# A two-layer graph attention kernel: reordering the first part and where Wr1 and the first residual products live

## The chip, the cores and the metric

The kernel runs on one core of one Trainium2 chip. Its time is the device time of one launch in microseconds (us), and the time of a kernel is the median over its runs. TensorE (PE) multiplies matrices; VectorE (DVE), ScalarE (ACT) and GpSimd (POOL) compute elementwise; SyncE (SP) only issues transfers. All have instruction queues of their own, which run in order.

## The reference

A graph has N = 3125 nodes with 768 features and E = 53125 edges, sorted by destination, with a self loop at every node.

```
h  = relu(layernorm(x))
# layer 1: 4 heads of 256
xl = h @ W1                                        # N x 1024
e  = leaky_relu((xl.a_src1)[src] + (xl.a_dst1)[dst], 0.2)   # per head
al = softmax of e over the edges that share a dst
g1 = segment_sum(xl[src] * al, dst) + b1
h1 = relu(layernorm(g1) * gamma1 + beta1) + (h @ Wr1 + br1)
# layer 2: the same with one head of 768 and W2, Wr2
out = x + layernorm(gat(h1)) * gamma2 + beta2 + (h1 @ Wr2 + br2)
```

## The kernel before, in words

Nodes are cut into 25 tiles of P = 125. Since the edges are sorted, the edges of a tile are a contiguous piece of the list; each tile gets S = 2304 slots, 18 chunks of 128, from its start in the list. `in_order` does the work in stages; `any_order` behind it is a fallback that runs only for a list that is not sorted. The Tile framework decides the order of instructions on each engine by priorities and inserts the waits; a buffer that is used again makes its new user wait for the old one.

1. `edge_list` (L188). The list `d_i` is loaded as 125 x 425. For each of 25 tiles DVE compares (L206) and ACT sums (L207), so that `cnt` holds how many edges lie below the tile; one product (L214) adds over partitions and gives `starts` (L219). The same function makes 16-bit copies of the list in HBM (`dst16_d`, and `slo16_d` for the source node modulo 125).
2. `fold` (L289). The attention vectors are folded into W1: POOL multiplies a 128-row chunk of W1 by a vector (L294), ACT sums over each head (L298) into `wa1`, so that h @ wa1 gives the node's attention terms.
3. `windows` (L236). For each tile SP reads its start and issues three transfers: destinations and sources as 32-bit numbers (`wd`, `ws`, L248 and L250) and 16-bit destinations (`k16`, L252). Seven tiles at a time are cast (L255) and transposed on PE (L257) into slot layout (L258). Then come gather indices, `hi_s` (source divided by 125) and `keep`.
4. Node tiles. Statistics (L313, L315, the square root on ACT L318, L321), normalisation, six transposes on PE (L570), ReLU into `h0` (L572), the next rows fetched, six products with `wa1` (L577, "alphas"), copied to `asad1` (L579).
5. `softmax` (L327) works in slot layout. Per tile it makes one-hot matrices on DVE from broadcast lists `bd` and `bs` (L359, L362, L365, L367), picks terms with PE (L377, L385), and then does segment maxima and sums by scans over rows. Meanwhile PE multiplies h0 by W1 (L588), ACT copies to `row` (L590), and SP stores `table1` and `h0T_d` (the transposed h0, by groups of four tiles).
6. Layer 1, in the pools "w2", "g1" and "e1". SP loads Wr1 (`wr1`, L601), the bias as two parts (`parts_of`, L149: load `v`, DVE splits off `lo`, SP stores it into row 1 of `b_r`, L164; four steps for 1024 columns), W2, and `h0k` (L614) from `h0T_d`. `residual(0)` (L624) computes the first group's residual h @ Wr1 and stores it to `r1T_d`. Then `sums` (L460) gathers one row of `table1` per slot (L477), weights it on ACT and DVE (L495, L496), adds by one-hot products on PE (L500, L512) over the bias product (L472), and ends each tile with `z` (L523). The fold of W2 (L294, L300) and `residual(1)` to `residual(6)` are handed to it as `later()`, a step per chunk.
7. Softmax and sums of layer 2 in the same manner; neither is touched except that both layers share the functions.

## Time and profile before

| what | value |
|---|---|
| runs | 2603.16, 2606.36, 2614.51 us; median 2606.36 |
| profiled execution | 2586.37 us, span 2584.5 us |
| mean granted PE clock of it | 0.936 |
| busy: PE, DVE, POOL, ACT | 2271.2, 1887.8, 1313.7, 1311.2 us |
| moved by DMA | 638.09 MB, mean 247 GB/s |
| first transpose of a node tile | 65.06 us |
| last copy of alphas | 144.22 us |
| first softmax product | 174.52 us |
| `residual(0)` on PE | 555.19 to 597.9 us |
| `z` of the first tile of layer 1 | 631.1 us |

How to read it: each engine's busy time is the sum of its instructions; PE's weight loads (PEld) run beside its products. In a line of the timeline the first two numbers are the start and the length in us, then come engine, line and operation, what is written from what, the size, how many (x), and in brackets how long the engine stood idle before it and which event ended that. A line of windows gives, for a stretch, its length and the busy time of PE, PEld, DVE, ACT and POOL with the number of instructions, then the granted clock of PE, the DMA share and GB/s.

### The profile page before, as it was taken

The numbers are of one execution on the slowest core, as the hardware profiler recorded it, in microseconds if no ns is written. First come the engines' busy times: TensorE is split into PE (matmuls) and PEld (weight loads), VectorE is DVE, ScalarE is ACT, GpSimd is POOL, SyncE is SP. The second block draws the span as 40 slices with busy tenths as digits, with TensorE's granted clock in tenths as the row PEclk, the third lists the DMA queues.
The fourth block names the chain that finished last, engine by engine and source line by source line (L and its number), as shares of the span: only waits on it lengthen the run. The fifth ranks groups of instructions, "written<-read, shape, count | busy, mean of one in ns | idle before, by whom it ended". The sixth has DMA issues, their size and how long they took to land. (4 is left out here: it accounts for less than half of the span.)

```text
span 2584.5 us, 35850 instructions
## 1 busy us (share of the span) xinstructions
PE 2271.2 (88%) x11226; PEld 1494.1 (58%) x11226; DVE 1887.8 (73%) x4289; ACT 1311.2 (51%) x2834; POOL 1313.7 (51%) x1007
## 2 busy tenths in 40 slices
PE   0969999949999999999999997768998889899786
PEld 0846654415666666666666675554575666566554
DVE  3559996027888988888888897785167768777776
ACT  5313321116788878888788894001044444444443
POOL 5100000047667667666676771002067778777875
PEclk9989999969999999999999998768999999999888
DMA  4228721177888888888888896773178988888886
GB/s 153 85 91 296 253 87 58 52 253 244 282 288 314 302 309 309 285 317 298 314 305 282 317 339 233 272 262 129 52 239 298 311 300 294 285 286 279 295 281 225
DMA packets 185428, 638.09 MB, mean 247 GB/s; under 512 B 31215, under 2 KB 50036, under 8 KB 184334
## 3 DMA queue, kind: packets, MB, share of 16 engines
q0 software_dynamic: 104032, 420.88, 47.7%
q1 hardware_dynamic: 76484, 202.08, 22.5%
q10 hardware_dynamic: 4714, 12.75, 1.4%
q8 instruction: 92, 1.51, 0.2%
q14 instruction: 106, 0.87, 0.1%
HBM read 566.11 MB, written 69.49 MB: 246 GB/s over the span
## 5 line engine op out<-in xcount | busy, mean ns | idle before, releaser
L477 POOL DMA_INDIRECT g<-table,idx_s x900 | 1196.8, 1330 | 1130.9 <-DVE oh L488 415.4
L495 ACT ACTIVATE hi<-g,al 128x256 fp32r<-128x256 f32 (+1 forms) x1925 | 970.9, 576 | 598.0 <-PE pa L500 275.0
L496 DVE SCALAR_TENSOR_TENSOR g<-g,al,hi 128x256 fp32r<-128x256 f32 (+1 forms) x1925 | 987.4, 564 | 126.8 <-ACT hi L495 124.4
L500 PE MATMUL pa<-hi,oh 128*125 128x512 f32 (+1 forms) x1450 | 581.0, 482 | 17.8 <-ACT hi L495 9.7
L500 PE MATMUL pa<-g,oh 128*125 128x512 f32 (+1 forms) x1450 | 459.4, 394 | 48.9 <-DVE g L496 48.4
L500 PEld LDWEIGHTS pa<-hi,oh 128*125 128x125 f32 x1450 | 270.5, 194 | 192.6 <-ACT hi L495 76.2
L500 PEld LDWEIGHTS pa<-g,oh 128*125 128x125 f32 x1450 | 269.7, 193 | 125.6 <-DVE g L496 86.2
L624 PE MATMUL pr<-h0k,wr 128*128 128x500 f32 (+1 forms) x672 | 300.7, 545 | 1.0 <-DMA h0k<-h0T_d 1.0
L717 PE MATMUL pr<-wr,h 128*125 128x384 f32 x800 | 299.3, 513 | 0.0
L677 PE MATMUL p<-w,h1T 128*125 128x384 f32 (+1 forms) x800 | 295.7, 489 | 1.8 <-DVE h1T L668 1.8
L512 PE MATMUL pa<-g,w 128*125 128x384 f32 (+1 forms) x900 | 291.8, 456 | 3.8 <-ACT w L510 3.0
L588 PE MATMUL pm<-w,h 128*125 128x512 f32 x600 | 274.7, 605 | 0.0
L512 PEld LDWEIGHTS pa<-g,w 128*125 128x125 f32 x900 | 171.7, 194 | 85.1 <-issue 27.8
L488 DVE TENSOR_SCALAR oh<-iota_f,rel_s 128x128 fp32r<-128x128 f32 x775 | 199.0, 286 | 20.1 <-PE pa L500 18.9
L717 PEld LDWEIGHTS pr<-wr,h 128*125 128x125 f32 x800 | 153.8, 197 | 92.1 <-issue 16.0
L677 PEld LDWEIGHTS p<-w,h1T 128*125 128x125 f32 x800 | 150.0, 188 | 72.8 <-DVE h1T L668 2.2
L588 PEld LDWEIGHTS pm<-w,h 128*125 128x125 f32 x600 | 110.0, 191 | 118.8 <-issue 118.8
L624 PEld LDWEIGHTS pr<-h0k,wr 128*128 128x128 f32 x672 | 124.9, 192 | 66.6 <-issue 22.8
L377 PE MATMUL pq<-tabs,ohs 125*128 125x100 bf16 (+1 forms) x2700 | 110.6, 198 | 43.4 <-DVE ohs L365 41.8
L377 PEld LDWEIGHTS <-ohs 125*128 125x128 bf16 x2700 | 105.5, 102 | 61.1 <-DVE ohs L365 54.3
L518 DVE TENSOR_TENSOR iso<-ao,node_f 125x1 f32<-125x1 f32 x50 | 7.8, 156 | 160.1 <-DMA ao<-alo_d,at_last 160.1
L590 ACT ACTIVATE row<-pm 125x512 f32<-125x512 f32 x50 | 29.8, 597 | 169.7 <-PE pm L588 159.2
(173 smaller groups left out, 1710.8 us busy)
## 6 DMA issues: line engine op xcount, KB each, us to landing
bd<-dst_d SPq DMA_DIRECT2D x50, 576.0 KB
bs<-slo_d SPq DMA_DIRECT2D x50, 576.0 KB
g<-table,idx_s POOLq DMA_INDIRECT x900, 5.9
r1T_d<-rt SPq DMA_DIRECT2D x100, 125.0 KB
r1t<-r1T_d SPq DMA_DIRECT2D x25, 500.0 KB
h1T_d<-h1T SPq DMA_DIRECT2D x25, 500.0 KB
h<-h1T_d SPq DMA_DIRECT2D x25, 500.0 KB
own<-table SPq DMA_DIRECT2D x24, 512.0 KB
```

The lines of the kernel that those rows point to most:

```text
L377: nc.tensor.matmul(q[:, j], ohs[:P, (j0 + j) * 128:(j0 + j + 1) * 128], tabs[:, i], start=(i == 0), stop=(i == 2))
L477: nc.gpsimd.indirect_dma_start(out=gf, out_offset=None, in_=table[:, :], in_offset=bass.IndirectOffsetOnAxis(ap=idx_s[:, c:c + 1], axis=0))
L488: nc.vector.tensor_scalar(oh, iota_f, rel_s[:, c:c + 1], None, op0=OP.is_equal)
L495: nc.scalar.activation(hi[:, cs], gf[:, cs], AF.Copy, scale=a)
L496: nc.vector.scalar_tensor_tensor(g[:, cs], gf[:, cs], a, hi[:, cs].bitcast(F32), op0=OP.mult, op1=OP.subtract)
L500: nc.tensor.matmul(pa[:, i, :f], oh[:, :P], t[:, i * f:(i + 1) * f], start=False, stop=(j == J - 1 and t is g))
L512: nc.tensor.matmul(pa[:, o // f, o % f:o % f + n], w[:, o // cols, :], gf[:, o:o + n], start=False, stop=(j == J - 1 and (o + n) % f == 0))
L588: nc.tensor.matmul(pm, h0[gi][:, k, o:o + P], w1[:, k, i * 512:(i + 1) * 512], start=(k == 0), stop=(k == NK1 - 1))
L590: nc.scalar.activation(row[:, i * 512:(i + 1) * 512], pm, AF.Copy)
L624: nc.tensor.matmul(pm[:, :nb * P], wr1[:, k, m * 128:(m + 1) * 128], loaded[gi, k][:, :nb * P], start=(k == 0), stop=(k == NK1 - 1))
L677: nc.tensor.matmul(pm[:, :n], hT[:, k, :], w2[:, k, o:o + n], start=(k == 0), stop=(k == NK2 - 1))
L717: nc.tensor.matmul(pm[:, :384], h1[:, k, :], wr2[:, k, i * 384:(i + 1) * 384], start=False, stop=(k == NK2 - 1))
```

## The change

- The counts: one DVE instruction with a running sum (`accum_out`) per tile instead of a comparison on DVE and a sum on ACT.
- Four node tiles (`EARLY = 4`) are written ahead of the rest of the list work: their rows x0 and x1 are fetched ahead of the list, W1 is loaded half by ACT's and half by POOL's queue, eight row buffers instead of twelve. `transposed` and `alphas` are separate functions; alphas lag four tiles behind.
- `windows` stands ahead of `fold` in the program, takes sources from a 16-bit copy `src16_d`, and transposes 25 x 128 pieces, 18 per list, with two transfers per tile.
- `folded` gives the two vectors and one or two product buffers in one tile. For layer 1 that tile is in the room "wr1" of pool m1; the softmax's scratch (`scr`) and then Wr1 itself take the same room. Inside the softmax `pick`, `ohh`, `le`, `xs` and `fw` are views of the scratch, and `alo` is a view of `own`.
- `residual(0)` is replaced by products straight from `h0[0]` behind the table's products, with `copy_residual` for its ACT pass and stores; group 0 is neither stored to `h0T_d` nor read back.
- The pools w2, g1 and e1 are opened with `reuse_waits="tile"`.

```
@@ edge_list
+        s16 = ep.tile([P, F], I16, name="s16")
+        nc.vector.tensor_copy(s16, s_i)
+        nc.sync.dma_start(src16_d.rearrange("(p f) -> p f", f=F), s16)
...
-            nc.vector.tensor_scalar(less, d16, float(b * P), None, op0=OP.is_lt)
-            nc.scalar.activation(less, less, AF.Copy, accum_out=cnt[:, b:b + 1])
+            nc.vector.tensor_scalar(less, d16, float(b * P), 0.0, op0=OP.is_lt, op1=OP.add,
+                                    accum_out=cnt[:, b:b + 1])
@@ windows
-                for k in range(n):
-                    st = start_of(b0 + k)
-                    nc.sync.dma_start(wd[k * J:(k + 1) * J, :],
-                                      dst[ds(st, S)].rearrange("(j p) -> j p", p=128))
-                    nc.sync.dma_start(ws[k * J:(k + 1) * J, :],
-                                      src[ds(st, S)].rearrange("(j p) -> j p", p=128))
-                    nc.sync.dma_start(k16[b0 + k:b0 + k + 1, :], dst16_d[ds(st, S)][None, :])
...
+            for b in range(NB):
+                st = start_of(b)
+                nc.sync.dma_start(k16[b:b + 1, :], dst16_d[ds(st, S)][None, :])
+                nc.sync.dma_start(s16[b:b + 1, :], src16_d[ds(st, S)][None, :])
+            for t, to in ((k16, dst_s), (s16, src_s)):
+                tf = ep.tile([NB, S], F32, name="tf")
+                nc.vector.tensor_copy(tf, t)
+                pt = pe.tile([128, 512], F32, name="pe")
+                for j in range(J):
+                    nc.tensor.transpose(pt[:, j * NB:(j + 1) * NB], tf[:, j * 128:(j + 1) * 128], ident[:NB, :NB])
...
@@ folded, fold
+        t = tmp.tile([128, 2 + room, heads * cols], F32, tag=tag, name="ab")
...
-                t = tmp.tile([128, heads, cols], F32, name="at", bufs=1 + act)
+                t = abs_[2 + m % (len(abs_) - 2)]
@@ softmax
+                first = scr()
...
-                xs = sr.tile([R, S], F32, name="xs")
-                fw = sr.tile([R, S], F32, name="fw")
+                rows = scr() if scr else sr.tile([128, 2 * S], F32, name="rows")
+                xs, fw = rows[:R, :S], rows[:R, S:2 * S]
@@ layer 1, before the table
-            for k in range(NK1):
-                nc.scalar.dma_start(w1[:, k, :], W1[k * 128:(k + 1) * 128, :])
...
+                    for b in range(2):
+                        fetch(b)
+                    listed = edge_list(ep, pp)
+                    next(listed)
+                    for k in range(NK1):
+                        (nc.scalar, nc.gpsimd)[k % 2].dma_start(w1[:, k, :], W1[k * 128:(k + 1) * 128, :])
+                    for b in range(2, AHEAD):
+                        fetch(b)
+                    abs1 = folded(mp, H, C1, a_src1, a_dst1, "wr1", 2)
+                    for b in range(EARLY):
+                        transposed(b)
+                    for _ in listed:
+                        pass
+                windows(pp)
+                for _ in fold(abs1, w1, NK1, H, C1, wa1, True):
+                    pass
+                for b in range(EARLY, NB):
+                    transposed(b)
+                    alphas(b - EARLY)
+                for b in range(NB - EARLY, NB):
+                    alphas(b)
@@ the table and behind it
+                wr1 = mp.tile([128, NK1, HC], F32, tag="wr1", name="wr1")
+                for k in range(NK1):
+                    nc.sync.dma_start(wr1[:, k, :], Wr1[k * 128:(k + 1) * 128, :])
...
-                    if b % GB == GB - 1 or b == NB - 1:
+                    if gi and (b % GB == GB - 1 or b == NB - 1):
                         nc.sync.dma_start(h0T_d[gi][:, :, :o + P], h0[gi])
+                for m in range(NK2):
...
+                        nc.tensor.matmul(pm[:, :GB * P], wr1[:, k, m * 128:(m + 1) * 128], h0[0][:, k, :],
+                                         start=(k == 0), stop=(k == NK1 - 1))
+                    copy_residual(0, rt, pm, m, GB)
...
-            for k in range(NK1):
-                load(0, k)
-            abs2 = folded(wp, 1, C2, a_src2, a_dst2)
-            for _ in residual(0):
-                pass
+            for k in range(NK1):
+                load(1, k)
+            abs2 = folded(wp, 1, C2, a_src2, a_dst2, "ab", 1)
```

## Prediction

> **What bounds the kernel now.** I read the page first, then busy time by stage (windows), then the list of waits and the timeline at each place where TensorE stands still. L-numbers are those of the kernel before.
>
> ```profile
> PE 2271.2 (88%) x11226; PEld 1494.1 (58%) x11226; DVE 1887.8 (73%) x4289; ACT 1311.2 (51%) x2834; POOL 1313.7 (51%) x1007
> PE   0969999949999999999999997768998889899786
> PEclk9989999969999999999999998768999999999888
> ```
>
> PE is busy 88% of the span. A digit stands for 64.6 us. The low ones ahead of layer 1 are the first (0 to 65 us), the third (129 to 194) and the ninth (517 to 582). So the kernel is PE-bound with holes, and a change of the first part can shorten holes. The stages in numbers (columns: stretch, sum of its length, busy PE, PEld, DVE, ACT, POOL, granted clock, DMA share, GB/s):
>
> ```profile
> 0.00:25.00 25.00, 0.00 (x0) 0.00 (x0) 13.73 (x36) 4.49 (x12) 10.13 (x17) 1.00 0.89 299
> 25.00:65.00 40.00, 0.25 (x2) 0.09 (x2) 9.21 (x37) 32.83 (x139) 23.17 (x10) 1.00 0.17 60
> 145.00:175.00 30.00, 15.79 (x57) 7.09 (x55) 12.58 (x33) 0.00 (x0) 0.00 (x0) 0.81 0.17 57
> 500.00:525.00 25.00, 14.59 (x35) 6.04 (x33) 2.53 (x11) 3.06 (x7) 4.81 (x4) 0.88 0.35 121
> 525.00:550.00 25.00, 1.18 (x2) 0.49 (x2) 8.55 (x25) 6.60 (x16) 10.61 (x11) 0.50 1.02 353
> 700.00:1400.00 700.00, 700.00 (x2527) 456.79 (x2526) 593.38 (x1656) 575.52 (x1465) 472.61 (x329) 1.00 0.87 303
> ```
>
> Three holes: 65 us at the start, about 14 us before 175, about 40 us after 515. From 700 to 1400 PE is full, so a us taken out ahead of that comes off the end. What ends each hole (timeline):
>
> ```profile
> 37.55 23.17 POOL L294 TENSOR_TENSOR at<-w,ab 128x1024 f32<-128x1024 f32 x10 [13.01 <-issue]
> 64.08 0.16 DVE L321 RECIPROCAL bn_rs<-bn_sd 125x1 f32<-125x1 f32 x1 [25.32 <-ACT bn_sd L318]
> 65.06 1.49 PE L570 MATMUL pt<-ident,xt 125*128 125x125 f32 x6 [28.95 <-issue]
> 144.22 0.17 DVE L579 COPY asad<-pas 125x8 f32<-125x8 f32 x1 [2.60 <-PE pas L577]
> 174.52 0.63 PE L385 MATMUL pd<-tabd,ohd 125*128 125x24 bf16 x18 [13.72 <-DVE ohd L359]
> 546.21 1.18 PE L472 MATMUL pa<-b_r,ones_r 2*125 2x512 f32 x2 [31.62 <-DMA b_r<-lo]
> 555.19 5.02 PE L624 MATMUL pr<-h0k,wr 128*128 128x500 f32 x6 [0.95 <-DMA h0k<-h0T_d]
> ```
>
> Hole 1: ACT does 25 counts (L207) to 35.8, then the fold's 48 sums (L298) to 62.3, and only then the first `bn_sd`; PE's first transpose follows at 65.06. Hole 2: the slot lists and softmax tables stand between the last alphas (144.22) and the first softmax product. Hole 3: bias parts `b_r`, then `h0k` read back from HBM, then residual(0) until 597.9; the first real product of layer 1 (L500) starts at 597.38, 82.8 us after the last L588 product (514.6).
>
> **The change, part by part.**
>
> *Counts.* A count is now one DVE instruction with a running sum; 25 ACT passes (0.55 + 0.19, cadence 0.54) go. The trace shows no such DVE form. Lower bound: L206 without a sum, 0.27. Nearest row with a sum over the same 125x425: TENSOR_REDUCE L210, 0.58. The Trainium skill ("VectorE: DVE Perf Modes", section on two Vector instructions with no wait between them) says an op that also writes its accumulator is two instructions, which speaks against the change; the trace has a separate accumulator read only on ACT (0.19), so the upper bound is 0.77. I take 0.6. With 24 counts behind the statistics of tiles 2 and 3, whose rows land at some 25 to 27 us, `starts` comes at about 33.4 + 24c: 40 (c = 0.27), 47.8 (0.6), 52 (0.77). Before it was 36.6. So by itself the list part becomes later by some 11 us; by the rule, 15.
>
> *Loads.* x0 and x1 now go ahead of the list in SP's ring; W1 goes half by ACT, half by POOL. The first 25 us run at 299 GB/s, share 0.89. The skill ("DMA: Bandwidth & Descriptors", Issuing engines are not separate DMA queues) says that all issuers end on the same 16 engines: the trace agrees that the start is filled, so I give the second queue nothing (an issue-time view would give some 2 us), and the list lands at 16 to 18 instead of 10. That is in the 33.4 above. POOL's x rows 8 to 11 wait for tiles 0 to 3 and stand ahead of the fold; those tiles are done by some 30 us, before the fold may run anyway.
>
> *Four tiles first, and fold order.* In ACT's order the square root of tile 4 stands ahead of all 48 fold sums, and tile 4's statistics stand on DVE just behind `starts`. So the fold begins at about starts + 2.2, and costs what it did: 35.73 to 62.3, 26.6 us (10 POOL products of 2.31 and their sums). End F = 47.8 + 2.2 + 26.6 = 76.6, later than 62.3 by 14. But PE is not idle meanwhile: the transposes of tiles 0 to 3 and 25 instructions of L588 (0.85 each, 21 us) run under it. In both kernels 42 L588 instructions lie before the softmax. After F remain 21 transposed tiles at 0.68, 25 alphas at 1.23 and 17 L588 at 0.85: 14.3 + 30.8 + 14.5 = 59.6, of which the four first alphas run partly as the fold ends; with 1 to 2 us of latency the last alpha is copied at about F + 58 = 135. Before: 144.2. So −9 (c = 0.27: −17; c = 0.77: −5).
>
> *Slot lists.* SP issued three DMAs per tile from 37.9 to 121.7 (2.17 us per tile, the last tiles later, behind two buffers); now two, 1.6 us or so, from 50 to some 95: hidden in both. On PE the last L257 transpose waited behind 24 L588 instructions (149.5 to 159.8), and `hi_s` was ready at 167.67, the first `ohd` at 173.49 behind the `bd` DMA. New tail after the last alpha: cast of 25x2304 about 1.36 (L268 has that size: 1.34), 18 transposes 2.0, copy 0.65, and the same again, then the division 5.4 and the DMA 3.7: some 17.7 against 29.3 before. So −11.6. What could spoil it: the casts wait for the alphas only by DVE order; the 36 transposes stand in a row on PE with nothing between. First part together: −9 −11.6 = about −20; bounds −8 to −30.
>
> *Softmax.* Its buffers become views of one scratch that is later Wr1's room. From the first L385 product to the last L588 one PE has the same instructions in the same order: 340.1 us, carried over at nothing. Cover needed: Wr1's 6 loads wait on SP, between table stores, until the scans release the scratch; the `row` buffers (two) bridge the some 8 to 10 us. Without that cover L588 would stall by that much, and DVE's 25.00 of 25 in that stage leaves no room; I count 0 (0 to +10).
>
> *Transition.* residual(0) now multiplies straight out of `h0[0]` behind the last L588, without any load: 48 instructions, 42.7 us as before (555.19 to 597.9). Six `h0k` reads and one 1.5 MB store of h0T_d go (hidden: 0). SP's order sets the rest: four sets of r1T_d stores, the last at t + 42 (t is the last L588 product), then the four steps `v` load, `lo`, `b_r` store. In before these steps took 521.9 to 552.2, 30 us, under 353 GB/s of gathers and loads. Now the ten gathers have landed by then, and only w2 (3.1 MB) and h0k stand between: 13 to 18 us. First L500 at t + 43.5 + 15 = t + 58.5, before t + 82.8: −24. Bounds: steps as slow as before, −9; steps hidden, −40. This new wait is a real one: PE stands still from t + 43 to t + 58, and what is late next is w2, whose loads stand in the same ring.
>
> *Start of layer 1.* The fold's 16 POOL products stood in one block ahead of gather 11 (561.2 to 604.2); now they alternate with gathers: 1.33 + 1.7 = 3.0 per chunk against 2.25 (40.4/18) needed, for 16 chunks. Ten gathered chunks cover 10 × 1.9 us; chunk 26 would come at 56 us and be wanted at 55. Before, blocks 1 and 2 took 45.9 and 41.7 instead of 40.4. I take −2 (−8 to +8).
>
> **Sum.** −20 −24 −2 = −46 on the profiled run, 2586.4 to 2540. That run lies 20 us (0.8%) under the median of the three shown and under all of them, so the same step from 2606.4 gives 2561. By the accumulator rule at its full price it would be 2565.
>
> **The rivals.**
> *A, the first part gains nothing* (chance 0.12). The list is later, the fold is tied to it by one small square root, and PE fills with L588, which is only brought forward. For: ACT's order. Against: hole 2's L588 queue goes in any case. The gain of the first part vanishes when F reaches some 97, that is `starts` at 68. Then 2606 − 26 = 2580.
> *B, all hides* (0.16). Counts near 0.3, the bias steps quick, early layer 1 fluent: −30 −37 −8 = −75, 2531.
> *C, it does not do what it says* (0.07). The bias steps behind the r1T stores take as long as before and the first part gives nothing: −9, 2597.
> *D, slower by the clock* (0.07). With holes shortened PE runs denser, and the granted clock, 1.00 through 700:1400 but 0.81 and lower in the first 200 us, drops in the layer. 1% of the 850 us of filled layer is 8.5 us; from 5.4% on it eats the 46 us; at 7% the time is 2606 − 46 + 60 = 2620. Against: the clock was 1.00 where PE was fullest, and lowest where it was idle.
>
> **How the numbers follow.** The main case has 0.58: 2561, its own range 2541 to 2590. A and B are faster too, so faster by over 0.5% (13 us, about what a measurement of this kernel can tell from no change) is 0.86; C is the same, 0.07; D slower, 0.07. For 8 in 10 the range takes in B and A and nearly C: 2528 to 2600.
>
> **What would show it.** Right: L588 records on PE before 40 us; `starts` at 45 to 52, the fold's last sum at 72 to 80; last `asad` copy near 135, first `pd` product near 153; the last L588 near 494; residual(0) at once behind it, then a PE wait of 10 to 18 us on `b_r<-lo`; first z about 45 us sooner than 631. Wrong: counts above 1 us, a fold that ends past 97, a stall of L588 on its row copies, a b_r wait of 30 us, or a clock below 0.97 between 700 and 1400.

## The result and the profile after

The changed kernel is faster, by less than half of what was forecast. Its median is 2594.02 us over 8 runs (2586.81 to 2600.16), that of the kernel before on the same chip 2608.78 over 8 (2603.16 to 2614.51). The medians differ by 14.8 us; the ratio is 0.9929, interval 0.9909 to 0.9949, or about −18 us, where the working gave −46. The time lies in the range of 2528 to 2600; by the ratio the forecast step is 2.5 times too large.

The profiled execution took 2587.07 us (span 2585.2, mean granted clock 0.928). Lines of the page: busy time, PE's busy tenths, and PE's granted clock, in slices of 64.6 us.

```profile
PE 2283.1 (88%) x11254; PEld 1500.0 (58%) x11254; DVE 1933.8 (75%) x4303; ACT 1294.2 (50%) x2783; POOL 1298.1 (50%) x1010
PE   4859999978999999999999996778998989898766
PEclk9869999989999999999999997778999989899888
```

The first slice is no longer empty (4 instead of 0), the ninth went from 4 to 7, but the third is a 5, where it was a 6. The stages (stretch, length, busy PE, PEld, DVE, ACT, POOL, granted clock, DMA share, GB/s):

```profile
0.00:25.00 25.00, 1.63 (x8) 1.66 (x9) 6.68 (x25) 2.47 (x5) 4.46 (x14) 1.00 0.89 304
25.00:65.00 40.00, 28.42 (x82) 12.99 (x80) 40.00 (x89) 18.44 (x78) 25.09 (x15) 0.91 0.19 60
145.00:175.00 30.00, 11.95 (x140) 11.48 (x140) 22.85 (x42) 4.43 (x4) 0.00 (x0) 0.50 0.43 149
500.00:525.00 25.00, 25.00 (x60) 11.19 (x59) 0.00 (x0) 3.07 (x5) 11.08 (x12) 1.00 0.56 189
525.00:550.00 25.00, 20.73 (x50) 9.12 (x48) 3.35 (x14) 6.06 (x14) 0.33 (x1) 1.00 0.39 125
700.00:1400.00 700.00, 699.48 (x2535) 457.00 (x2534) 602.56 (x1682) 581.51 (x1484) 478.99 (x334) 1.00 0.87 305
```

PE works 28.4 of the 40 us from 25 to 65 (before: 0.25), and from 525 to 550 it works 20.7 instead of 1.2. The filled layer is as full as before, and its clock is 1.00. Timeline, with the new line numbers (L571 transposes of node tiles, L581 alphas, L583 their copy, L622 the table products, L634 residual(0), L478 the bias product, L663 the later residuals):

```profile
30.47 0.83 PE L571 MATMUL pt<-ident,xt 125*128 125x125 f32 x6 [1.01 <-issue]
50.47 20.84 POOL L292 TENSOR_TENSOR ab<-w,ab 128x1024 f32<-128x1024 f32 x9
73.10 0.59 PE L581 MATMUL pas<-wa,h 128*125 128x8 f32 x2 [4.03 <-ACT ab L297]
146.58 0.17 DVE L583 COPY asad<-pas 125x8 f32<-125x8 f32 x1 [2.84 <-PE pas L581]
166.12 0.63 PE L390 MATMUL pd<-tabd,ohd 125*128 125x24 bf16 x18 [11.41 <-issue]
505.33 40.40 PE L634 MATMUL pm<-h,wr 128*128 128x500 f32 x96
556.14 1.18 PE L478 MATMUL pa<-b_r,ones_r 2*125 2x512 f32 x2 [10.41 <-DVE g L502]
563.41 2.04 PE L663 MATMUL pr<-h0k,wr 128*128 128x500 f32 x2 [6.08 <-DMA h0k<-h0T_d]
```

The fold ends at 73 instead of 62.5; the last alphas are copied at 146.6, where 144.2 was measured before and about 135 was forecast. residual(0) follows the table products without a gap, and then come the two waits of hole 3, 10.4 and 6.1 us in place of 31.6.

Two single profiles of a kernel can differ by more than the change is worth. The table therefore gives the lengths of the stages in the first pair of profiles and in a second pair, for which both kernels ran again on one chip (c3_before_again, c2_after_again).

| stage, us | before | after | c3 (before) | c2 (after) | change, 1st / 2nd pair | forecast |
|---|---|---|---|---|---|---|
| start to first `pd` product | 174.5 | 166.1 | 175.8 | 165.8 | −8.4 / −10.0 | −20 |
| to the last table product | 340.1 | 339.4 | 340.8 | 338.5 | −0.7 / −2.3 | 0 |
| to layer 1's first `hi` product | 82.8 | 60.6 | 83.3 | 60.3 | −22.2 / −23.0 | −24 |
| to layer 1's last `z` | 984.3 | 992.3 | 986.0 | 991.8 | +8.0 / +5.8 | −2 |
| to layer 2's first `z` | 322.6 | 332.8 | 327.3 | 331.2 | +10.2 / +3.9 | none |
| to layer 2's last `z` | 669.9 | 683.4 | 670.1 | 670.7 | +13.5 / +0.6 | none |

The first pair gives nothing in sum (+0.4), the second −25. Most of the difference is the last row, whose instructions no edit touches: in the 16 profiles of this study it ranged from 658.6 to 689.9, with 658.6 and 670.1 for the same kernel before. That row is taken as scatter, which is not shown in full: in each of the five groups of runs on one chip that hold both kinds, kernels in which layer 2's `alo` is a view took longer there than those in which it is a tile of its own, by 0.6 to 13.5 us. The other five rows are the case: the transition came nearly as forecast, the first part gave half, and the last two lost.

### The profile page after: what moved, and what is told of

It is laid out like the page before. It is cut to its first block, busy times and chain, and to the rows that moved or that the text cites. A ratio compares the mean times of both kernels' runs of the same rounds, so it can differ in the third digit from the quotient of the medians.

```text
span 2585.2 us, 35765 instructions
## 1 busy us (share of the span) xinstructions
PE 2283.1 (88%) x11254; PEld 1500.0 (58%) x11254; DVE 1933.8 (75%) x4303; ACT 1294.2 (50%) x2783; POOL 1298.1 (50%) x1010
## 5 line engine op out<-in xcount | busy, mean ns | idle before, releaser
L483 POOL DMA_INDIRECT g<-table,idx_s x900 | 1173.2, 1304 | 1131.4 <-PE pm L634 397.3
L502 DVE SCALAR_TENSOR_TENSOR g<-g,al,hi 128x256 fp32r<-128x256 f32 (+1 forms) x1925 | 1007.1, 574 | 105.2 <-ACT hi L501 73.3
L506 PE MATMUL pa<-hi,oh 128*125 128x512 f32 (+1 forms) x1450 | 571.3, 476 | 18.2 <-ACT hi L501 8.4
L506 PE MATMUL pa<-g,oh 128*125 128x512 f32 (+1 forms) x1450 | 471.1, 400 | 58.6 <-DVE g L502 32.8
L749 PE MATMUL pr<-wr,h 128*125 128x384 f32 x800 | 305.8, 522 | 0.0
L622 PE MATMUL pm<-w,h 128*125 128x512 f32 x600 | 277.2, 610 | 0.0
L663 PE MATMUL pr<-h0k,wr 128*128 128x500 f32 (+1 forms) x576 | 257.0, 534 | 6.1 <-DMA h0k<-h0T_d 6.1
L622 PEld LDWEIGHTS pm<-w,h 128*125 128x125 f32 x600 | 110.3, 192 | 119.8 <-issue 119.7
L382 PEld LDWEIGHTS <-ohs 125*128 125x128 bf16 x2700 | 106.8, 103 | 62.5 <-DVE ohs L370 56.1
L663 PEld LDWEIGHTS pr<-h0k,wr 128*128 128x128 f32 x576 | 105.1, 190 | 48.5 <-DMA h0k<-h0T_d 6.8
```

The source lines that it names most:

```text
L382: nc.tensor.matmul(q[:, j], ohs[:P, (j0 + j) * 128:(j0 + j + 1) * 128], tabs[:, i], start=(i == 0), stop=(i == 2))
L483: nc.gpsimd.indirect_dma_start(out=gf, out_offset=None, in_=table[:, :], in_offset=bass.IndirectOffsetOnAxis(ap=idx_s[:, c:c + 1], axis=0))
L502: nc.vector.scalar_tensor_tensor(g[:, cs], gf[:, cs], a, hi[:, cs].bitcast(F32), op0=OP.mult, op1=OP.subtract)
L506: nc.tensor.matmul(pa[:, i, :f], oh[:, :P], t[:, i * f:(i + 1) * f], start=False, stop=(j == J - 1 and t is g))
L622: nc.tensor.matmul(pm[:P], h0[gi][:, k, o:o + P], w1[:, k, i * 512:(i + 1) * 512], start=(k == 0), stop=(k == NK1 - 1))
L663: nc.tensor.matmul(pm[:, :nb * P], wr1[:, k, m * 128:(m + 1) * 128], loaded[gi, k][:, :nb * P], start=(k == 0), stop=(k == NK1 - 1))
```

## The experiments

Line numbers differ from kernel to kernel by a few; the ratios are each against the kernel before on the same chip. The intervals of e1, e2, e5, e6 and e10 overlap the changed kernel's 0.9909 to 0.9949 (e4's touches it), so for these the lengths of stages are the evidence, each from one profile. "t" is the end of the last table product.

**c1_before_again**: the kernel before once more, one profile.

> The kernel before, unchanged, for a second profile. Layer 2's sums, from the first z to the last, took 669.9 us in the profile of before and 683.4 in that of the changed kernel, with the same instructions. Theory R (run to run): that stage scatters by 10 us and more between executions; then this profile shows something between 672 and 685, and a time 10 to 25 us above the first profile's 2586.4. Rival C: the change lengthens the stage; then it is 668 to 672 again.

It took 2575.64 us, and layer 2's sums 658.6 us: below what either side had expected. Every stage up to layer 2 repeats within 1.2 us (last alphas 144.9, first `pd` 175.0, first `hi` 83.1 behind t); only layer 2's sums differ, by 11. So a difference of stages is good to about a microsecond ahead of layer 2, and no better than 12 in its sums.

**e1_fold_dve**: does GpSimd's fold hold the alphas back?

```
-                nc.gpsimd.tensor_tensor(t, w[:, k, :heads * cols], abs_[m], OP.mult)
+                (nc.vector if act else nc.gpsimd).tensor_tensor(t, w[:, k, :heads * cols], abs_[m], OP.mult)
```

> The changed kernel with one edit: the 12 products of the first fold (W1 by the attention vectors) run on DVE instead of POOL; ACT still sums. Theory P (port): in the changed kernel POOL's nine products in a row (50.5 to 71.3 us) hold off DVE, whose 16-bit cast of the list stands from 50.78 to 71.55; the statistics of the next tiles come late, so PE waits after the fold. Then here the cast takes under 1 us, the products about 1.1 us each, the fold's last sum falls at about 66 us (73.1 in the changed kernel), and the last alphas are copied about 58 to 62 us behind it, at 124 to 128 (146.6 in the changed kernel): 15 to 20 us faster than the changed kernel, some 30 to 38 faster than before. Rival G (gate): the fold's end alone gates the node tiles and DVE's standstill costs nothing; then the last alphas stay 73 us behind the last sum, at about 139, 7 us faster than the changed kernel.

Ratio 0.9906 (0.9869 to 0.9943). The fold ended at 68.0 instead of 73.1, but the last alphas came at 144.8: missed by both. PE's windows of e1 show why:

```profile
75.00:90.00 15.00, 15.00 (x106) 12.04 (x105) 9.02 (x30) 6.06 (x17) 3.22 (x6) 1.00 0.47 154
90.00:110.00 20.00, 19.74 (x123) 19.19 (x122) 11.56 (x37) 7.04 (x18) 3.23 (x6) 0.68 0.38 118
110.00:137.00 27.00, 26.74 (x132) 26.65 (x132) 10.56 (x35) 8.45 (x20) 0.00 (x0) 0.50 0.00 1
```

Once the table products (L622, 512 columns) allowed ahead of the softmax were spent, at about 91 us, only transposes and alphas of 8 columns were left. PE was busy 26.7 of 27 us and the granted clock fell to 0.50. A tile's six transposes took 1.49 instead of 0.81, its alphas 2.53 instead of 1.38. The faster fold had let PE spend the wide products earlier, and the clock took back what it gave.

**e4_filler**: e1, with one 504-column product beside the alphas of each tile, whose result is not used (512 less the 8 columns of the alphas; where an expectation says 496, it is this product).

```
-                    pa = pp.tile([P, 2 * H], F32, name="pas", bufs=1)
+                    pas = pp.tile([P, 512], F32, name="pas", bufs=1)
+                    pa = pas[:, :2 * H]
+                    nc.tensor.matmul(pas[:, 2 * H:], h0[gi][:, 0, o:o + P], w1[:, 0, 2 * H:512], start=True, stop=True)
```

> As the first experiment (first fold's products on DVE), and one product of 504 columns more for every tile's alphas, whose result nothing reads. Theory K (clock): PE's granted clock falls to 0.50 where only transposes and alphas of 8 columns run, and stays at 1.00 where a 512-column product stands among them; the changed kernel spends those ahead of the fold. Then here the clock from 95 to 145 us is 1.00 (0.50 in the first experiment), a tile's 12 alphas records take 1.5 us instead of 2.7, and although 25 products of 0.43 to 0.85 us are added (10 to 21 us), the last alphas come at 134 to 142, before the 144.8 of the first experiment. Rival: the clock falls there for another reason; then it stays at 0.50 and the last alphas come at 165 to 180.

Ratio 0.986 (0.9811 to 0.9909). The clock in e4:

```profile
75.00:90.00 15.00, 15.00 (x106) 11.98 (x104) 9.83 (x32) 5.21 (x16) 3.00 (x6) 1.00 0.55 169
90.00:110.00 20.00, 20.00 (x142) 16.22 (x142) 13.80 (x45) 7.75 (x22) 3.23 (x6) 1.00 0.37 115
110.00:137.00 27.00, 27.00 (x181) 21.18 (x180) 7.17 (x25) 5.69 (x15) 0.00 (x0) 1.00 0.00 1
```

With 25 products more, the last alphas come at 140.2, 4.6 us sooner than in e1: PE does more and is done earlier, because its clock stays at 1.00. In e8, e9 and e11, which have both edits too, the clock in 110:137 is 0.94, 1.00 and 1.00.

**e5_no_tail**: alphas follow the transposes two at a time instead of four tiles behind, so that none is left over for the end.

```
+                done = 0
                 for b in range(EARLY, NB):
                     transposed(b)
-                    alphas(b - EARLY)
-                for b in range(NB - EARLY, NB):
-                    alphas(b)
+                    for _ in range(2):
+                        if done < b:
+                            alphas(done)
+                            done += 1
+                alphas(NB - 1)
```

> The changed kernel with one edit: the alphas do not lag four tiles to the end; behind each new tile up to two sets of alphas are written until they have caught up, so one set is left at the end instead of four. Theory K (clock and one buffer): the four sets at the end run at clock 0.50 to 0.60 and one after the other, 10 us from 137 to 146.7; among transposes and L588 products they cost 1.23 to 1.5 each. Then the last alphas come at 139 to 142, the first softmax product at 159 to 162 (166.1), and the kernel is 4 to 7 us faster than the changed one. Rival: PE is full anyway and the same products only change places; then 145 to 147 and no difference in time.

Ratio 0.9926 (0.9898 to 0.9955), as the changed kernel. The last alphas came at 154.1: the clock stayed at 0.50 from 75 to 110, longer than in the changed kernel, where it rose at about 86. Both sides of the expectation missed, and with the clock back so much later the run cannot tell what the order of the alphas alone is worth. When the clock comes back is not the same in every kernel, even with PE's order unchanged: in e3 below, the same order up to the softmax woke at about 104 and ended the alphas at 153.9.

**e10_fill_only**: the added product alone, the fold on GpSimd as in the changed kernel.

> The changed kernel with one 496-column product, whose result is not used, beside every pair of alphas and nothing else (the first fold's products stay on GpSimd). It settles whether the clock alone makes the step that failed, the last alphas at 146 instead of 135. By the clock: granted clock 0.90 or more from 75 to 137 us, fold's end still 73 to 75, last alphas at 139 to 143 (e4, with the fold on VectorE: 140.2; the step's 59.6 us behind the fold, plus 25 added products of 0.4 to 0.5, minus what runs under the fold, gives 139 to 145 on the sum's terms), first pd product 158 to 162, ratio to the kernel before 0.988 to 0.993. If GpSimd's fold is what holds the alphas: last alphas at 145 or later though the clock is up.

Ratio 0.9953 (0.9937 to 0.9969), last alphas at 149.6. By its own numbers this went against the clock, but the expectation had a wrong term: the added product was put at 0.4 to 0.5 us and takes about 0.85 (1.01 with its overlap). The 24 of them behind the fold are 20 us instead of 10 to 12; without them the last alphas would be at about 129, an estimate. The windows show the clock and the price:

```profile
75.00:90.00 15.00, 15.00 (x71) 11.37 (x71) 7.39 (x23) 5.77 (x15) 1.94 (x4) 0.69 0.28 83
90.00:110.00 20.00, 20.00 (x144) 16.36 (x143) 13.53 (x45) 7.61 (x23) 3.65 (x8) 1.00 0.47 139
110.00:137.00 27.00, 27.00 (x191) 21.79 (x190) 12.90 (x42) 9.11 (x26) 1.46 (x3) 1.00 0.11 30
137.00:155.00 18.00, 18.00 (x82) 11.04 (x82) 3.45 (x7) 0.00 (x0) 0.00 (x0) 1.00 0.04 15
```

The clock is full from 90 on, and in 137:155 as well, where the changed kernel has 0.60; in 75:90 it is 0.69, short of the 0.90 expected. But in 90:137 the changed kernel's clock is 0.96 without the product, so there is little to win, and PE is full, so the product costs its whole length. Also 22 records of table products (9.69 us) come to stand ahead of the slot lists' transposes: from the last alphas to `pd` 26.5 us instead of 19.4. The product pays where the clock would else be at half, as behind the faster fold: 0.50 in 110:137 of e1, 1.00 in e4.

**e3_fold2_dve**: the second fold as one multiply-and-sum on VectorE, instead of a product on GpSimd between gathers and a sum on VectorE.

```
+                if not act:
+                    nc.vector.scalar_tensor_tensor(t, w[:, k, :cols], 1.0, abs_[m], op0=OP.mult, op1=OP.mult,
+                                                   accum_out=to[:, k, m:m + 1])
+                    continue
```

> The changed kernel with one edit: each of the 16 products of the second fold (W2 by its attention vectors) is one DVE instruction that multiplies and sums, so POOL has only gathers. Theory I (interleave): the products alternate with gathers 11 to 26 on POOL, 3.65 us a pair, so the first tile of layer 1 takes 55.5 us from its first product to z (33.7 before). Then here it takes 36 to 44, z of the first tile comes at 603 to 612 instead of 621.6, and at the end of layer 1 some 5 to 10 us are left of it. Rival D: DVE is as full in that tile (24.3 of 25 us), the longer DVE instruction costs what POOL saves, and z stays at 618 to 625, the time within 3 us of the changed kernel.

Ratio 0.9846 (0.9811 to 0.9882), the largest single gain. First GpSimd in the changed kernel, then VectorE in e3 (timelines):

```profile
575.56 0.98 POOL L483 DMA_INDIRECT g<-table,idx_s  x1
577.04 1.72 POOL L292 TENSOR_TENSOR ab<-w,ab 128x768 f32<-128x768 f32 x1 [0.49 <-DVE w L299]
578.91 0.98 POOL L483 DMA_INDIRECT g<-table,idx_s  x1
580.77 1.72 POOL L292 TENSOR_TENSOR ab<-w,ab 128x768 f32<-128x768 f32 x1 [0.89 <-DVE w L299]
582.64 0.97 POOL L483 DMA_INDIRECT g<-table,idx_s  x1
```

```profile
578.76 0.95 DVE L293 SCALAR_TENSOR_TENSOR ab<-w,ab 128x768 f32<-128x768 f32 x1
579.64 0.08 DVE L293 DVE_READ_ACCUMULATOR ab<-w,ab 128x1 f32 x1
```

In the changed kernel a gather comes every 3.4 to 4.0 us, since the one product buffer makes GpSimd wait for VectorE's sum too, and block 0 of layer 1 takes 55.5 us. In e3 it takes 38.6, and from t to the last `z` of layer 1 1028.8 us instead of 1052.9: −24, where 5 to 10 were expected to be left. The first tile's `z` came at 613.5, not at 603 to 612, since the alphas of this run ended 7 us later than in the changed kernel.

**e2_alo_own_tile**: the alphas' low parts of layer 2 in a tile of their own instead of a view of `own`.

```
-                alo = own.rearrange("p j v b -> p (j v b)")[:, :NB * J * (heads + 1)].rearrange(
-                    "p (b j c) -> p b j c", j=J, c=heads + 1)
+                if scr:
+                    alo = own.rearrange("p j v b -> p (j v b)")[:, :NB * J * (heads + 1)].rearrange(
+                        "p (b j c) -> p b j c", j=J, c=heads + 1)
+                else:
+                    alo = sr.tile([128, NB, J, heads + 1], F32, name="alo")
```

> The changed kernel with one edit: in layer 2's softmax the array alo is a tile of its own again, not a view of own. Theory A: as a view it frees the room of the first gathered rows sooner, so layer 2's first gathers start 0.8 us behind the last alo product instead of 5.4, run ahead of the small loads v of the bias, and PE waits 10.9 us for the bias product. Then here the gathers start some 5 us behind alo, PE's wait for the bias falls to 1 to 3 us, and the stage from the last sums of layer 1 to the first z of layer 2 is back from 332.8 to 322 to 325 us: 8 to 10 us faster than the changed kernel. Rival: the slow v loads of that one profile were chance; then the stage stays at 330 to 333 and the time is that of the changed kernel within 3 us.

Ratio 0.9906 (0.9874 to 0.9938). From the last `z` of layer 1 to the first of layer 2 324.0 us, against 328.9 and 333.3 in e1 and e3 on the same chip and 332.8 in the changed kernel. PE's wait ahead of layer 2's first tile, in the changed kernel and in e2:

```profile
1784.15 0.97 PE L478 MATMUL pa<-b_r,ones_r 2*125 2x384 f32 x2 [10.89 <-issue]
```

```profile
1771.12 0.75 PE L481 MATMUL pa<-b_r,ones_r 2*125 2x384 f32 x2 [2.03 <-DMA v<-in_L_gnn_b_dram]
```

The kernels with the change's view and its bias loads lie at 327.5 to 333.3 in this stage, those of before at 322.6 to 327.3, e2 and e11 at 324.0 and 325.5 (e7 to e9, whose bias loads differ, are left out). So the view costs some 6 us on the mean of these profiles; e2 beside the changed kernel's first profile gives 8.8, as expected. In the changed kernel the bias's loads `v` go out amid ten gathers; the second one is issued at 1766.32 and used at 1776.00:

```profile
1762.15 0.95 POOL L483 DMA_INDIRECT g<-table,idx_s  x1 [218.89 <-DVE xr L754]
1766.32 0.42 SPq L157 DMA_DIRECT2D v<-in_L_gnn_b_dram  x1
1776.00 0.27 DVE L163 CAST b_r<-v 1x256 fp32r<-1x256 f32 x1
```

In c1 the gathers begin at 1786.27, and the load issued at 1786.53 is used at 1790.21, after 3.7 us instead of 9.7.

**e6_bias_early**: e3, with the bias split ahead of W2, W2 and group 1's `h0k` on ACT's queue, and residual(0)'s stores on that queue too.

```
-            w2 = wp.tile([128, NK2, R2], F32, name="w2")
             b1_r = parts_of(b1, HC, wp, "b1")
             g1_c = by_chunk(g1, wp, NK2, "g1_c")
             be1_c = by_chunk(be1, wp, NK2, "be1_c")
+            w2 = wp.tile([128, NK2, R2], F32, name="w2")
...
-                nc.sync.dma_start(w2[:, k, :C2], W2[k * 128:(k + 1) * 128, :])
+                nc.scalar.dma_start(w2[:, k, :C2], W2[k * 128:(k + 1) * 128, :])
```

> The third experiment (second fold on DVE) with three edits more: the residual stores of the first group leave SP and go by ACT's queue, the bias parts and the vectors g and be lie in front of W2 in the pool, so that they no longer lie where h0[0] lies, and W2 and the first h0k go by ACT's queue, behind the residual. Theory B (a new wait): in the changed kernel the bias steps stand on SP behind the residual's stores and behind a load that waits for h0[0], so PE waits 10.4 us for the bias and 6.1 for h0k. Then here PE goes on with layer 1 within 2 us of the residual's end, the first product of layer 1 comes 43 to 48 us behind the last table product (60.6 in the changed kernel, 61.5 in the third experiment), and the end of layer 1 is 8 to 15 us sooner than there, counted from the last table product (1028.8 us). Rival: something else is late next, W2 on ACT or the gathers; then the first product comes sooner but the end of layer 1 by under 4 us.

Ratio 0.9884 (0.9837 to 0.9931), the first `hi` product at t + 64.8 (43 to 48 expected, 61.5 in e3) and the last `z` of layer 1 at t + 1043.3, worse than e3: missed by both sides. The first bias product is hardly waited for now (0.77 us), and `h0k` takes its place, behind W2 in the queue:

```profile
571.97 4.59 PE L667 MATMUL pr<-h0k,wr 128*128 128x500 f32 x6 [16.80 <-DMA h0k<-h0T_d]
```

**e7_one_load**: e3, the bias from one load into two partitions, its low part made in place, and `h0k` ahead of W2 (the first loads moved up, not shown).

```
+            v = tmp.tile([2, n], F32, name="v")
+            nc.sync.dma_start(v, bcast(vec, n, 2))
...
+            nc.vector.tensor_copy(r, v)
+            nc.vector.tensor_sub(v, v, r.bitcast(F32))
+            nc.vector.tensor_scalar(v, v, ident[0:2, 1:2], None, op0=OP.mult)
+            nc.vector.scalar_tensor_tensor(r, r.bitcast(F32), ident[0:2, 0:1], v, op0=OP.mult, op1=OP.add)
```

> e3_fold2_dve (second fold one multiply-and-sum on VectorE) with two more edits: the bias parts come from one load into both partitions and are separated with the identity's first two columns, so that no low part travels by a DMA; and the first h0k loads are issued ahead of W2. Measured of e3: first layer-1 product 61.5 us behind the last table product (513.4 to 574.9), layer 1's last projection done 1028.8 behind it, layer 2's first sum 333.3 behind that. Theory (the low parts' round trips and h0k's place behind W2 are what TensorE waits for): no wait of TensorE on the bias, a wait on h0k of at most 6 us, first product 46 to 52 us behind the last table product, layer 1's end 1013 to 1022 behind it; and in layer 2 the bias's loads, still behind the gathers, hold TensorE by some 4 us less, so 326 to 331. Rival (W2, now loaded last, is late next: VectorE's fold operations stand ahead of the first g products in its order and wait for W2): first product at 46 to 56 all the same, but layer 1's end 1026 to 1032, no gain. Ratio to the kernel before: 0.978 by the theory, 0.984 by the rival.

Ratio 0.9883 (0.9864 to 0.9902). Both of PE's waits are gone (first `hi` product at t + 43.5), and yet layer 1 ends at t + 1029.4, as in e3: the rival's number. The first five tiles end at t + 248.4, against 252.0 in e3. residual(0)'s 42.7 us and five blocks at the 39 us that later blocks take are 237 (an estimate), so e3 had left some 15 us to gain, and e7 has a new wait: PE stands 11.3 us for VectorE, which itself waits 11.7 us for the second fold's vectors, now loaded behind W2 (the rival had named W2 itself). Layer 2's first `z` came 340.5 us behind layer 1's last, where 326 to 331 were expected: PE stands 17.0 us ahead of layer 2's residual, as in e8 below. The alphas ended at 160.0 here, the clock being 0.50 from 75 to 110.

**e8_all**: e7 with the edits of e1, e2 and e4.

> All of it together: e7_one_load, with the low parts of layer 2's alphas in a tile of their own (e2_alo_own_tile), the first fold's products on VectorE (e1_fold_dve) and the extra 496-column product beside every pair of alphas (e4_filler). If the parts add: first product of node data 158 to 160 us (e4: 159.2), from there to the last table product 339 to 341, layer 1's end 1013 to 1022 behind that, layer 2's first sum 320 to 325 behind that, ratio to the kernel before 0.968 to 0.975. Rival (what is gained ahead of the softmax stage and at the layer's end is given back as waits on the gathers in layer 2): layer 2's sums take 15 us more than the 660 to 685 of the other runs, ratio 0.978 or more.

Ratio 0.9822 (0.9806 to 0.9838), short of the theory: the last `z` of layer 1 at t + 1029.2 (1013 to 1022 expected), layer 2's first 335.9 behind it (320 to 325). The two waits that came in with e7's edits are here too (timelines of VectorE and of PE):

```profile
573.90 0.96 DVE L291 SCALAR_TENSOR_TENSOR ab<-w,ab 128x768 f32<-128x768 f32 x1 [13.13 <-DMA ab<-in_L_gnn_a_src_dram]
1568.03 0.97 PE L753 MATMUL pr<-ball_r,ones_r 2*125 2x384 f32 x2 [16.86 <-issue]
```

The fold's vectors load behind W2, and VectorE stands for them with block 0's scaling behind it. In layer 2 the split of the summed bias `ball_r` is placed ahead of the softmax's products in PE's order, and PE stands 16.9 us there. (The rival named for this run, longer layer-2 sums, is not what the lines show.)

**e9_fold_late**: e8, the second fold behind 18 steps of residual(1).

```
+                first = residual(1)
+                for _ in range(J):
+                    yield next(first)
                 yield from fold(abs2, w2, NK2, 1, C2, w2[:, :, C2:], False)
-                for gi in range(1, NG):
+                yield from first
+                for gi in range(2, NG):
                     yield from residual(gi)
```

> e8_all with the second fold standing behind the first 18 steps of residual(1) instead of ahead of them, so that VectorE's fold no longer stands in its order ahead of block 0's scaling while its vectors and W2 are still on the way (in e8 VectorE waited 13.13 us for that load, and TensorE's block 0 took 56.6 us, 544.7 to 601.3). Theory (it is VectorE's place in the order, not the loads as such, that gave the gain of the early bias back): block 0 36 to 46 us, layer 1's last z 1012 to 1020 us behind the last table product (e8: 1029.2), ratio to the kernel before 0.974 to 0.980. Rival (the gathers, r1T stores and loads share the same DMA engines, so what is not waited for in block 0 is waited for in blocks 1 and 2): last z 1024 or more behind the last table product, ratio 0.981 to 0.984.

Ratio 0.985 (0.9824 to 0.9877). Block 0 fell to 46.2 us, but layer 1's last `z` stands at t + 1031.3: the rival's number (that the DMA engines are the reason is not shown). The vectors' load still ended late, and VectorE waited 13.1 us for it at 577.33; the edit moved the wait into block 0's end and did not remove it. Issuing those loads ahead of W2 was not tried.

**e11_parts_sum**: the changed kernel with e1, e2, e3 and e4, and nothing on the bias or the loads.

> The changed kernel with the four edits that helped alone, and without those on the bias and the loads: second fold as multiply-and-sum on VectorE (e3), alphas' low parts of layer 2 in a tile of their own (e2), first fold's products on VectorE (e1) and the extra product beside the alphas (e4). e8 and e9, with the bias from one load and h0k ahead of W2 as well, gave 0.982 and 0.985, no more than e3 alone (0.985), and in them TensorE stood 16.9 us ahead of layer 2's residual. If the four add: last alphas at 138 to 143, first pd 157 to 162, from the last table product to z of tile 4 252 to 256 us, from the last z of layer 1 to the first of layer 2 322 to 327, ratio 0.974 to 0.981. If what is taken out in one stage is lost in the next: ratio 0.982 or more, with the stage named by its length.

Ratio 0.9781 (0.9754 to 0.9808): 2546.85 us against 2604.62, −58 us, the fastest of all kernels here. Last alphas 140.7, first `pd` 159.7, the first five tiles of layer 1 at t + 250.6, layer 2's first `z` 325.5 behind layer 1's last. Every stage lies in its expected interval or better, so the four amounts add, as far as one profile tells. What e8 and e9 had in addition gave nothing in layer 1 (its last `z` at t + 1029.2 in e8, 1030.1 here) and cost 10 us ahead of layer 2 (335.9 in e8).

**c2_after_again, c3_before_again**: both kernels once more on one chip.

> The changed kernel once more, for its stages beside those of the kernel before on the same chip. If the layer-2 sums' length belongs to the chip and the run (659 to 672 us in one job, 684 to 690 in the others), they lie within 5 us of those of the kernel before here; if it belongs to the change, they are 12 us or more longer. The last alphas at 140 to 154 (the clock's return), the rest as in the first profile within 5 us.

> The kernel before once more, on the same chip as c2_after_again: last table product 514 to 516, last z of layer 1 1581 to 1583, from there to the first z of layer 2 322 to 324; layer-2 sums 655 to 690, as the chip gives it.

2570.58 and 2595.3 us. Layer 2's sums took 670.7 and 670.1, alike in this pair. In c3 t was 516.6, layer 1's last `z` 1585.9 and the stage behind it 327.3, each beyond its interval, the last by 3.3 us.

## Why the prediction was wrong in size

Right in direction, mechanism by mechanism:

- *Counts.* 0.60 and 0.08 for the accumulator's read, one every 0.515 us, against 0.6 taken; the pair of instructions that the Trainium skill names ("VectorE: DVE Perf Modes", section on two Vector instructions with no wait between them) is in the trace, but the second costs 0.08, not the 0.19 borrowed from ACT. `starts` came at 42.7, sooner than 47.8, and the fold's end at 73.1, sooner than 76.6, behind tile 4's square root on ACT as said.
- *Slot lists.* 19.4 us from the last alphas to `pd`; forecast 17.7 (its parts add to 17.1), before 30.1. This is all that the first part gained, since the last alphas came no sooner; on them rival A was right.
- *Softmax.* 339.4 for 340.1, carried over at nothing: right.
- *Transition.* First `hi` at t + 60.6, forecast t + 58.5. residual(0) took 40.4 us for 42.7. The b_r wait is 10.4 us (10 to 18 forecast); the line names a product of VectorE as its end, but with the bias's round trips gone, in e7, the wait is gone too. What was late next is `h0k`, 6.1 us, behind the w2 that was named.
- *Rival D*, a lower clock in the filled layer: 1.00 in 700:1400. It fell.

The step that failed is *Four tiles first*: "After F remain 21 transposed tiles at 0.68, 25 alphas at 1.23 and 17 L588 at 0.85 … about F + 58 = 135." Measured was F + 73.5. The sum prices all of PE's work behind the fold with durations from the part of before in which PE ran at full pace. But before, too, PE began that work at half pace: six transposes took 1.49 us at 65.06, a line that the prediction shows while it takes 0.68, and a tile's alphas came down from 2.53 to 1.37 only at 85 us:

```profile
79.48 2.53 PE L577 MATMUL pas<-wa,h 128*125 128x8 f32 x12
85.98 1.37 PE L577 MATMUL pas<-wa,h 128*125 128x8 f32 x12
```

(The windows give a clock of 1.00 there, but the first clock record in the trace of before stands at 85.3 us; ahead of it the durations decide.) At the prediction's prices the 25 transposed tiles, 25 alphas and 24 table products of before come to 68 us. They took 79, from 65.06 to 144.04. So the −9 set a measured time of before with some 10 us of half pace in it against a sum for the changed kernel with none, and the changed kernel has nearly as much. These rows are of the changed kernel:

```profile
62.50:75.50 13.00, 1.59 (x7) 1.32 (x7) 12.01 (x8) 10.58 (x47) 8.81 (x4) 0.61 0.03 8
75.00:86.00 11.00, 10.28 (x43) 9.04 (x43) 4.07 (x15) 3.01 (x8) 0.78 (x2) 0.50 0.05 15
86.00:137.00 51.00, 51.00 (x355) 40.84 (x354) 30.25 (x96) 19.49 (x53) 6.49 (x12) 0.97 0.29 95
137.00:147.00 10.00, 8.42 (x50) 7.99 (x49) 1.08 (x6) 0.36 (x1) 0.00 (x0) 0.68 0.00 0
```

```profile
78.41 2.69 PE L581 MATMUL pas<-wa,h 128*125 128x8 f32 x12 [0.26 <-DVE asad L583]
82.79 2.70 PE L571 MATMUL pt<-ident,xt 125*128 125x125 f32 x12
137.38 1.48 PE L581 MATMUL pas<-wa,h 128*125 128x8 f32 x12 [0.26 <-DVE asad L583]
143.89 2.65 PE L581 MATMUL pas<-wa,h 128*125 128x8 f32 x12 [0.35 <-DVE asad L583]
```

The missing 15 us, worked out from the timeline: at 0.50 from 75.5 to 86, half of it, 5; the first wait behind the fold, 2.4; the last four alphas, 9.4 us with gaps and at half clock in place of 4 × 1.23, 4.5; 18 table products at 0.94 and one slow pair, 3. Half pace is some 9 of these 15 (5 up to 86, 1.7 in the slow pair at 120, 2.5 in the last alphas; an estimate from the durations); the first wait, the gaps of a single `pas` buffer and the table products' longer step are the rest.

What goes with the low clock is shown in part. Under the fold PE stands waiting for ACT's sums. In all eight profiled kernels with the change whose first fold is on GpSimd, PE was busy 1.6 to 3.9 of the 13 us in 62.5:75.5, and the clock fell to 0.50 at 65 to 68 us. In the five with that fold on VectorE (e1, e4, e8, e9, e11) PE was busy all 13 and the clock there was 1.00. This row is of e1:

```profile
62.50:75.50 13.00, 13.00 (x67) 8.34 (x66) 10.19 (x28) 7.24 (x32) 1.07 (x2) 1.00 0.23 69
```

It is not enough to close that hole. In e1 the table products were spent by 91 us, and the narrow rest ran at half pace; with the added products of e4 it did not, and the alphas ended sooner. With the added products alone (e10) the hole under the fold stays, and nothing is gained. In the changed kernel itself table products stand with nearly every tile from 81 to 134 us, so a lack of them alone does not explain the half pace up to 86. The Trainium skill ("TensorE: Matmul & The Clock Gate", Part 1) sets the rate by how busy PE has been lately, with the full rate after about 3.4 us of sustained work. The fall under the fold agrees with it. The return does not: before, PE was busy 19.94 of 20 us in 65:85 at half pace, and in e1 26.74 of 27 us at 0.50. By the page the changed kernel would have lost some 2 us behind the fold (an estimate) instead of 5; the measured clock decides.

*Start of layer 1* was mis-sized: −2 taken, +8 and +5.8 measured, at the end of its bounds. The pair of gather and product was put at 3.0 us; with the wait for the sum that frees the single product buffer it was 3.4 to 4.0. Block 0 alone took 55.5 us for 33.7, so the first `z` came at 621.6, only 9.5 us sooner than before where 45 were forecast; the next blocks gave part of it back. e3 settled this.

*Layer 2's start* was not in the sum at all: "neither is touched except that both layers share the functions". The view that freed one tile brought the gathers forward, and the bias's loads behind them: some +6.

Sum by the runs: −9 (first part), −1.5 (softmax), −22.5 (transition), +7 (layer 1), +6 (layer 2's start) = −20, against −18 by the ratio and −14.8 by the medians. What the change may add in layer 2's sums is not in it.

## What to carry to other kernels

Beside your sum for a stage of the changed kernel, sum the same stage of the kernel before with the same durations: here that would have missed 11 of its 79 us, and this was the largest error of the forecast. Read a matmul's duration together with the granted clock of its stretch, and ask whether the change leaves in that stretch what kept the clock up: in e1 the wide products were spent early, and the narrow ones left behind ran at half pace. When an edit removes a wait, find the next load in the same queue and what stands behind its user in that engine's order before counting a gain; e6 to e9 each removed a wait and found another. And when functions are shared, follow a changed buffer into every stage that uses it.

## What the runs showed of the hardware

A cast from fp32 to 16 bits on VectorE took 0.37 us in e1, and in the changed kernel 20.77, from the moment at which GpSimd began nine products in a row until they ended:

```profile
50.78 20.77 DVE L237 CAST l<-slt 125x425 int16<-125x425 f32 x1
```

```profile
53.88 0.37 DVE L237 CAST l<-slt 125x425 int16<-125x425 f32 x1
```

It did not get in between two of them, and VectorE's next statistics stood behind it until 71.6. Whether this cost anything by itself was not separated: the fold ended at 73.1 all the same.

The granted clock stayed at 0.50 with PE busy without a gap: in e5 20.00 of 20 us in 90:110, with 512-column products between the narrow ones. It came back at about 86 us in the changed kernel and about 104 in e3, with the same order of work on PE up to there, and in the kernel before at about 85, some 20 us after PE had begun; why it differs was not found.
